# Routed transposes inside a second stage, a third first-layer PSUM buffer, moved loads and stores around the start of the dense stage, and a state copy on ScalarE, in a graph-network and expert kernel

## The chip, the cores and the metric

The kernel runs on one core of a Trainium2 chip. The core has five engines with an instruction queue each: TensorE (PE in the profile; its weight loads are shown apart as PEld), VectorE (DVE), ScalarE (ACT), GpSimd (POOL) and SyncE (SP), which here only issues DMAs. Matmul results go to PSUM, which has eight banks, and an engine must copy them out. The metric is the device time of one execution in microseconds (us), lower is better; the median of three runs is compared.

## The reference

The layer has two parts. A graph network on 128 graphs of 128 nodes with 256 features, and then a mixture of experts whose gate comes from graph attention over a million random edges. In short (N = 16384 nodes; reshapes left out):

```python
# part 1: graph network, D = 256, hidden 512
h = (1.0 + eps) * ln(x) + einsum('bnm,bmd->bnd', adj, ln(x))
x = x + relu(h @ W1 + b1) @ W2 + b2
# part 2: attention decides the experts
y = ln(x)
hg = (y @ W_gat).reshape(N, 4, 4)               # heads x experts
e = leaky_relu((hg * att_src).sum(-1)[src] + (hg * att_dst).sum(-1)[dst], 0.2)
ee = exp(e - segment_max(e, dst)[dst])
alpha = ee / (segment_sum(ee, dst)[dst] + 1e-16)
agg = segment_sum(hg[src] * alpha[:, :, None], dst) + b_gat
scores = ln(agg).reshape(N, 4, 4).mean(1)
top_s, top_i = top_k(scores, 2); w = softmax(top_s)
for ei in range(4):
    g = where(top_i == ei, w, 0).sum(-1)
    x = x + g[:, None] * (gelu(y @ W1[ei] + b1[ei]) @ W2[ei] + b2[ei])
```

Each node uses two of the four experts. All data are float32.

## The kernel before

**Stage 1** is the graph network. 32 tiles of four graphs are loaded, normalised, multiplied by their adjacency (L2091), sent through the first layer (`hidden`, matmul L2104, four blocks of 128 hidden units, two matmuls each, accumulated in a PSUM tile `p_hid` that ScalarE empties with a relu at L2108) and the second layer (`outputs`, L2115, sum on DVE at L2120), then normalised again and transposed (`turned`, L2134, also into `p_hid` tiles), and turned into the table of attention rows (`rows`, L2145). The pool `gnn_hid` holds two `p_hid` tiles. A framework schedules this stage: it orders the instructions of all engines itself. On DVE it mixes in `sort_edges`, which sorts the edges by target; its first loads are `sv` and `dv` (L226, L227) on SP's queue, and its first DVE instruction is L244.

**Stage 2** is written by hand: under `manual_schedule` the order in which the program issues instructions is the order on each engine. A small planner (`Plan`) decides this order at build time. It holds three lists of tasks, named pool, tensor and vector, each a Python generator that issues some instructions and then yields an assumed time in us, or a condition (`plan.after(us)`, `plan.was(name)`) before which it isn't to go on. The planner always steps the list whose assumed clock is furthest behind. `plan.done(name, after)` sets the time from which a condition holds. These are assumptions, nothing of them is measured on the chip: they decide order alone.

- The tensor task is `Experts.task`. Until `todo` is empty it runs 36 dense units (`dense`: tiles 23 to 31 with each of the four experts): first layer in `first` (L1614, gelu L1618), second layer in `second` (L1633, result copy on ScalarE L1640), store of the result `ys`. A unit's second layer is issued after the first layer of the next unit (`last`), so two units overlap.
- Then it runs 49 routed units. Each has two sets of 128 nodes, one set for each expert of a pair. POOL gathers their rows (`r_x`, L889), PE transposes them (`Routed.turn`, four instructions at L1760, into a tile of the pool `moe_big`), ScalarE copies the result to `m_xn` (L1764), and `Routed.load` issues the loads of the first-layer weights of the two experts on SP (L1731, L1737). `Routed.first` is the first layer (32 matmuls, L1779, gelu L1785); the second layer is again L1633 and L1640; DVE scales and adds (L1802, L1812), and POOL scatters the rows to the output (`put`, L896). `turn` does nothing if the planner doesn't yet hold the unit's rows to have arrived, if one transposed unit is already waiting, or if the list of the unit isn't there.
- The lists of nodes for the units come in five parts, of 11, 10, 10, 6 and 12 units, each built on DVE and PE from the gates of a part of the graphs (`lists`, matmuls L1440 and L1525).
- After each second layer `gathers.mark()` lets ScalarE copy a number into `marks` (L885). POOL copies it to `seen` (L880) before it issues further gathers, so that POOL doesn't run far ahead of PE.
- The vector tasks are the count of the edges (`count`, with the histogram at L738 to L776 and matmuls L761), the attention (`attend`, 13 blocks of edge rows), the sums at the ends of each node's edges (`ends`, `fetch`), and the gates (`pieces`). A block of `attend` does exponentials on ScalarE (L1141, L1142), products on DVE (L1146), a scan on DVE (L1154), a copy of the scan's states into row order on DVE (L1160), and stores of these rows on SP (L1163).

At the start of stage 2 the program issues, in this order: the load of the experts' second biases for all rows (`b2_rows`, 512 KB, L2202, SP), the first dense activations (`m_xn`, 512 KB, L1605, POOL's queue, since nothing is loaded yet), twelve small stores of zeros behind the ends of the state tables (L2237, SP); and with the first dense unit the activations of the second tile (SP).

Of the kernel before, what the change touches and what calls it, by code (L numbers as in the profile page):

```python
# [13 lines left out]
F32 = mybir.dt.float32  # L14
# [8 lines left out]
PSUM = bass.MemoryType.PSUM  # L23
DRAM = bass.MemoryType.DRAM

P = 128
D = 256
DH = 512
NB = 128
# [4 lines left out]
X = 4  # L34
# [32 lines left out]
TURN_US = 0.8  # L67
# [51 lines left out]
WIN = 16  # L119
# [17 lines left out]
ROW = 24  # L137
# [932 lines left out]
def attend(nc, c, plan, gathers, states, dst_t, aw, once, ps, ahead):  # L1070
# [11 lines left out]
    for k in range(NBL):  # L1082
# [8 lines left out]
        e = once.tile([P, H, CB + 1], F32, name="e")  # L1091
# [5 lines left out]
        else:  # L1097
            dt, st = before
# [21 lines left out]
        st = aw.tile([P, ROW, CB + 1], F32, name="state")  # L1120
# [36 lines left out]
        )  # L1157
        rows = once.tile([P, CB * ROW], F32, name="room")
        rows = rows.rearrange("p (c f) -> p c f", f=ROW)
        nc.vector.tensor_copy(rows, st[:, :, 1:].rearrange("p f c -> p c f"))  # L1160
        for (_, of), to in sorted(zip(PARTS, states), key=lambda v: v[0][1].stop):
            if of.start <= cols.start and cols.stop <= of.stop:
                nc.sync.dma_start(  # L1163
# [3 lines left out]
                    rows,  # L1167
                )
        before = (dt, st)
        yield 6.5  # L1170
        plan.done(f"states{k}", 4.0)


def finish_attention(nc, c, plan, name, graphs, hm, own, fin, aw):
# [411 lines left out]
class Experts:  # L1586
# [12 lines left out]
    def load(self, t, xn=None):  # L1599
        if t < NT and t not in self.loaded:  # L1600
            if xn is None:
                xn = self.mp.tile([P, 2, G * P], F32, name="m_xn")

            queue = self.nc.sync if self.loaded else self.nc.gpsimd
            queue.dma_start(xn, self.xn_d[t].rearrange("p (k n) -> p k n", k=2))  # L1605
            self.loaded[t] = xn

    def first(self, xn, w1, b1):
# [33 lines left out]
    def dense(self):  # L1642
        w = self.w
        t, e = self.todo.pop(0)
        self.load(t)
        if e == 0:
            self.load(t + 1)
        hid = yield from self.first(self.loaded[t], w.w1[:, e], w.b1[:, e])

        def second():  # L1650
            y = self.mp.tile([P, G, D], F32, name="m_out", bufs=3)
            yield from self.second(hid, [w.w2[:, e]] * 2, [w.b2[:, e]] * 2, y)
            self.stored.append((t, e))
            self.nc.sync.dma_start(self.ys[t, e], y.rearrange("p s d -> p (s d)"))
            self.plan.done(f"stored{t}-{e}", SECOND_US / G + 4.0)

        return second
# [8 lines left out]
    def task(self):  # L1666
        self.load(self.todo[0][0])
        yield self.plan.after(NET_US - 6.0)
        last = None
        while self.todo or last or self.routed is None or self.routed.left():  # L1670
            second = None
            self.ask()
            if not self.todo and self.routed and self.routed.turn():
                yield TURN_US
            if self.routed and self.routed.turned and not self.todo:
                second = yield from self.routed.first()
                if self.routed.turn():
                    yield TURN_US
            elif self.todo:
                second = yield from self.dense()  # L1680
            if last:
                yield from last()
                self.gathers.mark()
                yield SECOND_US / G
            elif not second:
                yield self.plan.after(0.5)
            last = second
# [149 lines left out]
def adj_ffn_kernel(  # L1837
# [22 lines left out]
    nc = tc.nc  # L1860
    ctx.enter_context(nc.allow_non_contiguous_dma(reason="weights, vectors and cells"))

    const = ctx.enter_context(tc.tile_pool(name="const", bufs=1))
# [6 lines left out]
    last = dram.tile([P, CB * ROW], F32, name="last")  # L1870
# [3 lines left out]
    states = [  # L1874
        dram.tile([NB * (cols.stop - cols.start) + WIN, ROW], F32, name=f"states{i}")
        for i, (_, cols) in enumerate(PARTS)
    ]
# [6 lines left out]
    c = Consts()  # L1884
# [70 lines left out]
    def layer_norm(work, xt, name):  # L1955
# [28 lines left out]
    right = ctx.enter_context(ExitStack())  # L1984
    mw = right.enter_context(tc.tile_pool(name="mw", bufs=1, side="right"))
    w = Consts()
# [1 line left out]
    w.ones3 = mw.tile([3, P], BF16, name="ones3")  # L1988
    nc.vector.memset(w.ones3, 1.0)
    w.b2 = mw.tile([3, X, D], BF16, name="mb2")  # L1990
    ps_one = right.enter_context(
        tc.tile_pool(name="ps_one", bufs=1, space=PSUM, side="right")
    )
    kept_pool = right.enter_context(ExitStack())
    kept = kept_pool.enter_context(tc.tile_pool(name="kept", bufs=1, side="right"))
    c.counted_raw = kept.tile([P, EC // 2], I32, name="counted")
# [12 lines left out]
    with tc.tile_pool(name="gw", bufs=1) as gw, tc.tile_pool(  # L2009
        name="gnn", bufs=2  # L2010
    ) as gp, tc.tile_pool(name="gnn_big", bufs=2, space=PSUM) as ps_big, tc.tile_pool(
        name="gnn_hid", bufs=2, space=PSUM
    ) as ps_hid, tc.tile_pool(name="gnn_small", bufs=1, space=PSUM) as ps_small:

        self_w = gw.tile([P, 1], F32, name="self_w")
# [83 lines left out]
        def hidden(h_t):  # L2099
            hid = gp.tile([P, DH // P, G * P], F32, name="hid")  # L2100
            for f in range(DH // P):
                p_hid = ps_hid.tile([P, G * P], F32, name="p_hid")
                for k in range(2):
                    nc.tensor.matmul(  # L2104
                        p_hid, w1_sb[:, k, f * P : (f + 1) * P], h_t[:, k, :],
                        start=(k == 0), stop=(k == 1),
                    )
                nc.scalar.activation(hid[:, f, :], p_hid, AF.Relu, bias=b1_sb[:, f : f + 1])  # L2108
            return hid
# [47 lines left out]
        for t in range(NT):  # L2157
            xt, h_t = sums
            hid = hidden(h_t)
            if t == 0:  # L2160
                load_row_weights()
            if t + 1 < NT:
                sums = gather_rows(*load(t + 1))
            if t > 1:
                xn_t = turned(t - 2, made.pop(0))
            x1 = outputs(t, xt, hid)
            made.append(x1)
            if t > 1:
                rows(t - 2, xn_t)
            if t == 12:  # L2170
                load_late(x1[:, 0, 0:1])
            if t == 24:

                zeros = const.tile([P, G, 2], F32, name="zeros")
                nc.vector.tensor_single_scalar(
                    zeros, x1[:, :, 0:2], 0.0, op=ALU.mult
                )
                for to in xr_tiles:
                    nc.sync.dma_start(to[:, :, 2 * D :], zeros)
        for t in (NT - 2, NT - 1):  # L2180
            rows(t, turned(t, made.pop(0)))

# [10 lines left out]
    with tc.tile_pool(name="moe", bufs=2) as mp, tc.tile_pool(  # L2193
        name="moe_big", bufs=2, space=PSUM
    ) as ps_big, tc.tile_pool(name="moe_hid", bufs=3, space=PSUM) as ps_hid, tc.manual_schedule(
        engines={ENG.DVE, ENG.Activation, ENG.PE, ENG.Pool}
    ):
        plan = c.plan = Plan()
        c.ps_big, c.ps_one = ps_big, ps_one
        first = mp.tile([P, 2, G * P], F32, name="m_xn")  # L2200
        w.b2_rows = mp.tile([P, X, D], F32, name="b2_rows", bufs=1)
        nc.sync.dma_start(w.b2_rows, b2[None].to_broadcast([P, X, D]))  # L2202
        tail = ExitStack()
        pool_fin = tail.enter_context(tc.tile_pool(name="fin", bufs=2))
        behind = tail.enter_context(ExitStack())
# [22 lines left out]
        def count():  # L2228
# [1 line left out]
            count_pool.close()  # L2230
            kept_pool.close()
            plan.done("counts")

        pad = const.tile([WIN, ROW], F32, name="no_rows")
        nc.gpsimd.memset(pad, 0.0)
        for to in states:
            nc.sync.dma_start(to[NB * (to.shape[0] // NB) :], pad)  # L2237

        def ends():

# [34 lines left out]
        def pieces():  # L2275
# [3 lines left out]
                tc.tile_pool(name="wins", bufs=2, side="right")  # L2279
            )  # L2280
            routes = Routes(nc, c, plan, fp, ps_one, xr)
            nc.sync.dma_start(hm, table[M - 1 : M, :].to_broadcast([P, ROW]))
            for i, graphs in enumerate(PIECES):
                n = graphs.stop - graphs.start
# [494 lines left out]
```

## Time and profile before

| | us |
|---|---|
| runs of the kernel before | 2299.92, 2304.63, 2306.51 |
| median | 2304.63 |
| the profiled execution | 2292.6 |
| its span (first to last instruction) | 2290.8 |
| mean clock granted to TensorE in it, as a share of full speed | 0.932 |

The profile is one execution. A group of instructions is shown by line, engine, operation, output and inputs by the program's names, and shape; then busy time in us and the mean of one in ns; then the idle time of the engine just before them and what ended most of it. Some groups that the change touches:

```profile
L1779 PE MATMUL m_phid<-m_xn,mw 128*128 128x256 f32 x1568 | 392.6, 409 | 108.3 <-ACT m_xn L1764 83.2
L1640 ACT COPY m_out<-big 128x1024 f32<-128x1024 f32 x85 | 86.0, 1012 | 559.1 <-PE big L1633 306.9
L2104 PE MATMUL p_hid<-h_t,w_sb 128*128 128x512 f32 x512 | 235.2, 608 | 21.5 <-ACT hid L2108 20.2
L2108 ACT ACTIVATE hid<-p_hid,b_sb 128x512 f32<-128x512 f32 x128 | 86.6, 681 | 67.4 <-PE p_hid L2104 67.0
L880 POOL COPY seen<-marks 128x1 f32<-128x1 f32 x85 | 26.0, 305 | 347.4 <-ACT marks L885 347.2
```

Read the first as: 1568 matmuls of the routed first layer were busy for 392.6 us, 409 ns each; PE idled 108.3 us just before them, and 83.2 of that ended when ScalarE finished writing `m_xn` at L1764.

The stretches of the span: stage 1 runs from 0 to 655, the dense units and the sort of counts from 662 to about 1027, the histogram with dense units beside it and the first gates from there to about 1301, and the routed units from 1301 to 2264. The last 27 us are result copies and sums.

### The profile page before, as it was taken

The page shows a single profiled execution, that of the slowest core. Times are in us where ns is not written, and L with a number is a line of the kernel's source. Part 1 is how long each engine was busy: PE and PEld are TensorE (multiplying, and loading weights), DVE is VectorE, ACT ScalarE, POOL GpSimd, SP SyncE. Part 2 cuts the span into 40 slices and gives each one's busy share as a digit, 9 for nine tenths or more (in the row PEclk, how much of TensorE's full clock was granted, in tenths as well). Part 3 has the DMA queues.
Part 4 walks back from the last instruction along what each step waited for, and adds up shares of the span by engine and source line. Part 5 has one row for each costly group of instructions (what it writes and reads, how often), then busy time and mean ns, then how long its engine had stood idle before and what let it go on. Part 6 is the DMA issues. An engine that isn't in the chain of part 4 may idle for free. (4 is left out here: it accounts for less than half of the span.)

```text
span 2290.8 us, 28852 instructions
## 1 busy us (share of the span) xinstructions
PE 1965.9 (86%) x8888; PEld 1466.4 (64%) x8888; DVE 1608.1 (70%) x4428; ACT 842.0 (37%) x1565; POOL 1050.6 (46%) x1011
## 2 busy tenths in 40 slices
PE   7999989988979998996698789776887977789996
PEld 4677767766756655664454468555676756667885
DVE  5889999958999998884344336464553565487877
ACT  6778545544422222322222324222232322324342
POOL 2111011101038887885455756555656654544431
PEclk9999999999979998998898899888998988899998
DMA  8898987898321122222113633453353533445866
GB/s 206 227 230 219 247 211 196 202 176 148 98 70 53 53 55 94 93 93 65 33 47 69 225 88 111 132 164 99 98 161 103 174 93 79 86 152 160 316 222 228
DMA packets 300935, 319.23 MB, mean 139 GB/s; under 512 B 112722, under 2 KB 238946, under 8 KB 300646
## 3 DMA queue, kind: packets, MB, share of 16 engines
q1 hardware_dynamic: 233030, 237.34, 33.3%
q0 software_dynamic: 67744, 79.96, 17.8%
q8 instruction: 75, 1.23, 0.2%
q14 instruction: 86, 0.70, 0.1%
HBM read 165.04 MB, written 128.04 MB: 128 GB/s over the span
## 5 line engine op out<-in xcount | busy, mean ns | idle before, releaser
L889 POOL DMA_INDIRECT hs<-table,index x552 | 624.5, 1131 | 168.0 <-issue 164.1
L1633 PE MATMUL big<-mw,m_hid 128*128 (+1 forms) x2720 | 647.3, 393 | 52.8 <-issue 52.2
L1633 PEld LDWEIGHTS big<-mw,m_hid 128*128 128x128 f32 x2720 | 524.7, 196 | 150.2 <-issue 80.8
L1779 PE MATMUL m_phid<-m_xn,mw 128*128 128x256 f32 x1568 | 392.6, 409 | 108.3 <-ACT m_xn L1764 83.2
L1779 PEld LDWEIGHTS m_phid<-m_xn,mw 128*128 128x128 f32 x1568 | 316.7, 205 | 169.0 <-ACT m_xn L1764 89.5
L1640 ACT COPY m_out<-big 128x1024 f32<-128x1024 f32 x85 | 86.0, 1012 | 559.1 <-PE big L1633 306.9
L1614 PE MATMUL m_phid<-m_xn,mw 128*128 128x512 f32 x576 | 264.1, 609 | 24.5 <-ACT m_hid L1618 12.2
L1785 ACT ACTIVATE m_hid<-m_phid,r_b 128x256 f32<-128x256 f32 x392 | 161.8, 472 | 309.7 <-remote 116.3
L2104 PE MATMUL p_hid<-h_t,w_sb 128*128 128x512 f32 x512 | 235.2, 608 | 21.5 <-ACT hid L2108 20.2
L2033 POOL DMA_DIRECT2D at<-in_adj_dram x31 | 41.0, 1324 | 432.3 <-DMA at<-self_eye 426.8
L2115 PE MATMUL big<-w_sb,hid 128*128 128x256 f32 x1024 | 228.8, 381 | 0.0
L2115 PEld LDWEIGHTS big<-w_sb,hid 128*128 128x128 f32 x1024 | 192.4, 191 | 24.6
L1614 PEld LDWEIGHTS m_phid<-m_xn,mw 128*128 128x128 f32 x576 | 110.9, 195 | 149.4 <-issue 127.6
L880 POOL COPY seen<-marks 128x1 f32<-128x1 f32 x85 | 26.0, 305 | 347.4 <-ACT marks L885 347.2
L2104 PEld LDWEIGHTS p_hid<-h_t,w_sb 128*128 128x128 f32 x512 | 94.9, 193 | 136.1 <-issue 98.2
L1618 ACT ACTIVATE m_hid<-m_phid,mb 128x512 f32<-128x512 f32 x144 | 97.5, 687 | 144.0 <-PE m_phid L1614 97.9
L889 POOL DMA_INDIRECT r_x<-xr,nodes x98 | 106.5, 1087 | 66.4 <-issue 42.8
L1540 DVE TENSOR_SCALAR low<-wide,part 128x128 bf16<-128x128 bf16 x332 | 61.3, 260 | 92.7 <-remote 34.2
L896 POOL DMA_INDIRECT out_dram<-r_x,places x98 | 105.3, 1074 | 35.0 <-issue 21.3
L1812 DVE SCALAR_TENSOR_TENSOR r_x<-m_out,r_x 128x256 f32<-128x256 f32 x196 | 90.6, 483 | 33.5 <-ACT m_out L1640 24.8
L2108 ACT ACTIVATE hid<-p_hid,b_sb 128x512 f32<-128x512 f32 x128 | 86.6, 681 | 67.4 <-PE p_hid L2104 67.0
L1802 DVE SCALAR_TENSOR_TENSOR r_x<-b_rows,r_x 128x256 f32<-128x256 f32 x196 | 90.5, 483 | 10.5 <-issue 4.8
(405 smaller groups left out, 2614.5 us busy)
## 6 DMA issues: line engine op xcount, KB each, us to landing
mw<-in_L_ffn_W_dram SPq DMA_DIRECT2D x106, 512.0 KB
states<-room SPq DMA_DIRECT2D x54, 552.0 KB
ys<-m_out SPq DMA_DIRECT2D x36, 512.0 KB
y_in<-ys SPq DMA_DIRECT2D x36, 512.0 KB
xt<-in_x_dram SPq DMA_DIRECT2D x32, 512.0 KB
xt<-b_sb POOLq DMA_DIRECT2D x32, 512.0 KB
x_d<-x SPq DMA_DIRECT2D x32, 512.0 KB
xn_d<-xn_t SPq DMA_DIRECT2D x32, 512.0 KB
```

What stands on the lines that cost most here:

```text
L889: self.nc.gpsimd.indirect_dma_start(out=out, out_offset=None, in_=rows, in_offset=bass.IndirectOffsetOnAxis(ap=index, axis=0),)
L896: sc = self.nc.gpsimd.indirect_dma_start(out=rows, out_offset=bass.IndirectOffsetOnAxis(ap=index, axis=0), in_=values, in_offset=None, bou ...
L1614: nc.tensor.matmul(p_hid, w1[:, k, f * P : (f + 1) * P], xn[:, k, :], start=(k == 0), stop=(k == 1),)
L1618: nc.scalar.activation(hid[:, f, :], p_hid, AF.Gelu, bias=b1[:, f : f + 1])
L1633: nc.tensor.matmul(p_y[:, s, :], hid[:, f, s * P : (s + 1) * P], w2[s // 2][:, f, :], start=(f == 0 and not b2), stop=(f == DH // P - 1 an ...
L1779: nc.tensor.matmul(p_hid[:, half], w1[i][:, k, f * P : (f + 1) * P], xt[:, k, :], start=(k == 0), stop=(k == 1),)
L1785: nc.scalar.activation(hid[:, f, half], p_hid[:, half], AF.Gelu, bias=b1[i][:, f : f + 1])
L1802: self.nc.vector.scalar_tensor_tensor(x[:, s, D : 2 * D], b2[i], x[:, s, 2 * D + i : 2 * D + i + 1], x[:, s, D : 2 * D], op0=ALU.mult, op1 ...
L1812: self.nc.vector.scalar_tensor_tensor(x[:, s, D : 2 * D], y[:, 2 * i + s, :], x[:, s, 2 * D + i : 2 * D + i + 1], x[:, s, D : 2 * D], op0= ...
L2104: nc.tensor.matmul(p_hid, w1_sb[:, k, f * P : (f + 1) * P], h_t[:, k, :], start=(k == 0), stop=(k == 1),)
L2108: nc.scalar.activation(hid[:, f, :], p_hid, AF.Relu, bias=b1_sb[:, f : f + 1])
L2115: nc.tensor.matmul(p_y[:, s, :], hid[:, f, s * P : (s + 1) * P], w2_sb[:, f, :], start=(f == 0), stop=(f == DH // P - 1),)
```

## The change

- In `Experts.task`, while a second layer is issued (`last`), the transposes of the next routed unit are tried after every quarter of it (`routed.turn()`), where before they were tried only before and after a first layer.
- The pool `gnn_hid` of stage 1 has three tiles in place of two. The PSUM bank for it comes from `ps_one`, which was opened before stage 1 and is now opened at the start of stage 2.
- The first dense activations are loaded on SP's queue. `b2_rows` is loaded in `pieces`, once the counts are done. The second tile's activations are loaded with the second dense unit and not with the first.
- The zeros behind the state tables are written in stage 1, in the program at the tile with number 24, where its framework places them as it sees fit.
- In `attend` the copy of the states into row order moves from VectorE to ScalarE. The planner issues it 4.6 + 1.5 us after the scan by its own clock, where before it followed the scan at once, and holds the stores as done 5.5 us after that.

```diff
@@ attend
-        nc.vector.tensor_copy(rows, st[:, :, 1:].rearrange("p f c -> p c f"))
+        yield 4.6
+        yield plan.after(1.5)
+        nc.scalar.copy(rows, st[:, :, 1:].rearrange("p f c -> p c f"))
...
-        yield 6.5
-        plan.done(f"states{k}", 4.0)
+        plan.done(f"states{k}", 5.5)
@@ Experts.load
-            queue = self.nc.sync if self.loaded else self.nc.gpsimd
-            queue.dma_start(xn, self.xn_d[t].rearrange("p (k n) -> p k n", k=2))
+            self.nc.sync.dma_start(xn, self.xn_d[t].rearrange("p (k n) -> p k n", k=2))
@@ Experts.dense
-        if e == 0:
+        if e == 1:
             self.load(t + 1)
@@ Experts.task
             if last:
-                yield from last()
+                for us in last():
+                    yield us
+                    if not self.todo and self.routed and self.routed.turn():
+                        yield TURN_US
                 self.gathers.mark()
@@ adj_ffn_kernel, before stage 1
-    ps_one = right.enter_context(
-        tc.tile_pool(name="ps_one", bufs=1, space=PSUM, side="right")
-    )
@@ stage 1
-        name="gnn_hid", bufs=2, space=PSUM
+        name="gnn_hid", bufs=3, space=PSUM
...
                 for to in xr_tiles:
                     nc.sync.dma_start(to[:, :, 2 * D :], zeros)
+                pad = const.tile([WIN, ROW], F32, name="no_rows")
+                nc.gpsimd.memset(pad, 0.0)
+                for to in states:
+                    nc.sync.dma_start(to[NB * (to.shape[0] // NB) :], pad)
@@ stage 2
+        ps_one = right.enter_context(
+            tc.tile_pool(name="ps_one", bufs=1, space=PSUM, side="right")
+        )
         plan = c.plan = Plan()
...
-        nc.sync.dma_start(w.b2_rows, b2[None].to_broadcast([P, X, D]))
...
-        pad = const.tile([WIN, ROW], F32, name="no_rows")
-        nc.gpsimd.memset(pad, 0.0)
-        for to in states:
-            nc.sync.dma_start(to[NB * (to.shape[0] // NB) :], pad)
@@ pieces
             routes = Routes(nc, c, plan, fp, ps_one, xr)
+            nc.sync.dma_start(w.b2_rows, b2[None].to_broadcast([P, X, D]))
             nc.sync.dma_start(hm, table[M - 1 : M, :].to_broadcast([P, ROW]))
```

## The prediction

> **What bounds the kernel now.** I read the page's busy shares first, then the stretches of the span, then what TensorE (PE) waits for, and last the timeline where the routed units run.
>
> ```profile
> PE 1965.9 (86%) x8888; PEld 1466.4 (64%) x8888; DVE 1608.1 (70%) x4428; ACT 842.0 (37%) x1565; POOL 1050.6 (46%) x1011
> ```
>
> PE is busy for 86% of the span, VectorE (DVE) for 70%, ScalarE (ACT) for only 37%. The average hides that the limit changes. Columns below: stretch in us, its length, then busy us of PE, PE weight loads, DVE, ACT and POOL, the PE clock, the DMA share and GB/s.
>
> ```profile
> 100.00:216.00 116.00, 110.62 (x528) 80.80 (x527) 101.08 (x383) 91.35 (x170) 15.67 (x12) 1.00 0.91 231
> 655.00:662.00 7.00, 0.01 (x1) 0.04 (x1) 6.62 (x45) 0.00 (x0) 0.48 (x2) 0.50 0.66 222
> 662.00:1027.00 365.00, 354.60 (x1184) 219.39 (x1185) 342.74 (x420) 103.87 (x156) 301.74 (x235) 0.97 0.23 69
> 1027.00:1301.00 274.00, 211.28 (x1205) 137.45 (x1204) 110.92 (x474) 67.38 (x94) 153.34 (x160) 0.89 0.29 77
> 1301.00:1700.00 399.00, 314.36 (x1413) 259.32 (x1412) 208.36 (x700) 115.40 (x235) 231.31 (x240) 0.89 0.40 122
> ```
>
> In stage 1 (to 655) PE, DVE and DMA are all near full. Between 662 and 1027 PE and DVE are both over 93% busy: PE runs dense expert units, DVE sorts counts and does the attention blocks, and the histogram at 1027 (L761) needs both. From 1301 on the routed units run; there only PE is close to its limit, 79% busy, and what it waits for is time lost:
>
> ```profile
> PE m_phid L1779 <- ACT m_xn L1764: 83.2, 25, 12.0
> PE p_hid L2104 <- ACT hid L2108: 20.2, 13, 5.9
> PE m_phid L1614 <- DMA states<-no_rows: 10.8, 1, 10.8
> PE big L1760 <- DMA r_x<-xr,nodes: 1.9, 2, 1.3
> ```
>
> (Total us, times, longest.) The biggest wait that one name carries is the first layer of a routed unit waiting for ScalarE to copy the transposed rows. The timeline of PE shows its form, and what a covered one looks like:
>
> ```profile
> 2187.09 0.60 PE L1760 MATMUL big<-ident,r_x 128*128 128x128 f32 x4
> 2188.93 7.17 PE L1779 MATMUL m_phid<-m_xn,mw 128*128 128x256 f32 x32 [1.24 <-ACT m_xn L1764]
> 2195.95 0.60 PE L1760 MATMUL big<-ident,r_x 128*128 128x128 f32 x4
> 2196.38 7.07 PE L1633 MATMUL big<-mw,m_hid 128*128 x32
> 2203.29 7.07 PE L1779 MATMUL m_phid<-m_xn,mw 128*128 128x256 f32 x32
> ```
>
> At 2187 the transposes (L1760) stand directly before their first layer and PE waits 1.24 us; at 2195 a second layer (L1633, 7.07 us) lies between and nothing is waited for. The 1.24 is the queue on ScalarE: it finishes the previous unit's result copy (L1640, 1012 ns) before the row copy (L1764, 588 ns).
>
> **Term 1, transposes inside a second layer: −24.8.** The built program's order of instructions says how often each form occurs. Before, 27 of 49 transposes have no second-layer matmul between themselves and their first layer; after, 7. The other 20 get 8 to 32 of the 32 matmuls (1.7 us or more, at 7.07/32 each) between. 20 × 1.24 = 24.8 us. The 0.60 of the transposes stays. Bounds: 0, if the time returns as another wait, and 24.8. The long waits in the row of 83.2 (5.76, 5.89, 11.45, 6.95, 11.99) I leave as they are: at most of them DVE, ScalarE and PE stand still together just after a burst of row gathers on POOL, and a turned tile ready earlier doesn't move that. What moves along: ScalarE's row copy now stands ahead of L1640 in its queue, the two expert weight loads of each unit (L1737) are issued up to 7 us earlier at a DMA share of 0.40, and the mark that lets POOL gather on (L885) keeps its place.
>
> **Term 2, drains: +11.3.** In the built order, transposes that stand behind 64 second-layer matmuls and directly before their first layer (the next list's rows weren't yet due, so both open second layers were run off) go from 2 to 5. Three more places where PE has nothing in hand. The trace doesn't show these three, so bounds: 0, since waits for gathered rows are 1.9 us in all; and the longest wait, 11.99. A wait also costs clock, which the same lines show:
>
> ```profile
> 1639.51 8.82 PE L1779 MATMUL m_phid<-m_xn,mw 128*128 128x256 f32 x32 [3.30 <-ACT m_xn L1764]
> 1845.30 10.02 PE L1779 MATMUL m_phid<-m_xn,mw 128*128 128x256 f32 x32 [11.99 <-ACT m_xn L1764]
> ```
>
> After 3.30 us of idling the 32 matmuls took 8.82 against 7.17, after 11.99 they took 10.02: 1.7 and 2.9 us more. Each drain is thus worth between 0 and 11.99 + 2.9 − 1.24 = 13.6 (the 1.24 is already left in the 7). I take the short row, 3.30 + 1.7 − 1.24 = 3.8, three times, because rows were waited for so little: 11.3; bounds 0 and 41.
>
> The Trainium skill, "TensorE: Matmul & The Clock Gate", section "HAM oscillation — how this bites in real kernels", says that PE's clock halves after an idle stretch of more than about 3.4 us. It speaks against this change, which trades gaps too short to lose the clock for a few that are long enough. By it a wait of 3.30 would cost no clock, the drains 6.2 and the whole 5 us less; the row, 8.82 after 3.30, is the measurement and decides.
>
> **Term 3, third first-layer buffer: −5.** PE's waits for L2108 are 20.2 us in 13. The first eleven, before 216 us, come to about 14; one of 5.93 at 486 is too long for one buffer, worth two matmuls (2 × 608 ns), and keeps some 4.7. So PE can win up to 14 + 1.2 + the small ones, about 16. The end of stage 1 and the histogram wait for DVE as well, though, and DVE's sort ends at 661.5. Only if DVE comes earlier does this count. DVE's adds wait for PE, which speaks for; its waits for input tiles (40.9 us, 21 times) at a DMA share of 0.88 to 0.91 speak against. Bounds 0 and −14; I take −5, nearer the DMA row.
>
> **Term 4, the pad stores: +2.** Twelve stores that lay at 655 behind the first dense load move, in the built order, to the head of SP's queue, before the first edge loads.
>
> ```profile
> 655.51 7.17 SPq L2237 DMA_DIRECT2D states<-no_rows  x12
> 35.69 1.23 DVE L244 SCALAR_TENSOR_TENSOR code<-dv 128x1024 int32<-128x1024 int32 x1 [14.13 <-ACT dv L242]
> ```
>
> They take 7.17 us of SP. DVE already idles 14.13 us for the first edges (second line), and these can come up to 7.2 later; behind them on SP stand the next input tiles. DVE's built order puts node work of two tiles ahead of L244, which covers most. Bounds 0 and +7.2; +2.
>
> **Term 5, first dense load: 0.** PE idles 10.84 us before the first dense matmul at 662 while three loads of 512 KB share 222 GB/s. By bytes, one alone takes 0.52 MB / 222 = 2.4 us, three 7.1, so up to 4.7 can go. But in the built order the second activation tile and the bias rows are issued right behind the first, about 0.4 us apart, so they still overlap; and until 1027 DVE decides. Without that cover it would be worth −3. Bounds −4.7 and 0.
>
> The Trainium skill, "Trainium Kernel Development and Optimization", section "Key Constraints", has loads from SP, ACT and POOL share the same 16 engines, so that another queue saves only issue time. By it the move from POOL's queue to SP's is worth one POOL issue at most; the profile has it at 0.57 us, and the sum has 0.
>
> **Term 6, state copies to ScalarE: −3.4 + 2.** L1160 ran 13 times on DVE at 1135 ns. Three lie before 1027, where DVE is 94% busy (342.74 of 365) and hands over to PE without slack: 3 × 1.135 = 3.4. The other ten lie where DVE is 40 to 60% busy: nothing. On ScalarE a copy of 1104 columns by the row of L1640 (1012 ns for 1024) takes 1.1 us; ScalarE is 28% busy there, and three buffers of PE cover one delayed gelu. Its cover gone, when the copy reaches ScalarE before DVE's scan (L1154, 2117 ns) is done, gelu, the result copy and PE stand behind: up to 2.1 us a block, 27 in all; the planner spaces it by 6.1 us after the scan's issue, so I take 0. With PE reaching the histogram after about 342 instead of 347 us of dense work, 5 us of it come later, into a stretch where PE idles 63 of 274: between 0 and +5, +2 taken.
>
> **Sum.** −24.8 + 11.3 − 5 + 2 + 0 − 3.4 + 2 = −17.9. The profiled execution took 2292.6 (span 2290.8, 1.8 around it), so 2274.7 by it. It lies 12 below the median of the three runs, 2304.63; carried there, 2286.7, say 2287.
>
> **The rivals.**
> *Larger gain.* Drains cost nothing and stage 1 gives its 14: 2304.6 − 24.8 − 14 + 2 − 3.4 + 2 = 2266. For it: row waits of 1.9 us. Against: DMA at 0.9 and DVE at 88% in stage 1.
> *No change, the routed stage is paced elsewhere.* A routed unit takes (2264 − 1301)/49 = 19.7 us where PE's own work is 7.07 + 7.07 + 0.60 = 14.7. If POOL's gathers and the lists made by DVE set this pace, the 24.8 come back as longer waits and the drains are how they look. Left are −5 + 2 − 3.4 + 2 = −4.4: 2300. For it: the engines that stop together. Against: POOL itself waits 347 us for PE's marks (L880), so it follows PE.
> *Slower, the drains.* One mechanism: at the three new drains the next rows come late, since PE now arrives at the list boundary sooner than the list, and PE idles with its clock lost. At 13.6 each, 41: −24.8 + 41 − 4.4 = +11.8, 2316. It decides from (24.8 + 4.4)/3 = 9.7 a drain, a wait of some 8.2 us. For it: waits of 11.45 and 11.99 are there already. Against: they are stops of all engines.
> *It doesn't do what it says.* The first load isn't alone in the built order; that is in term 5.
>
> **How the numbers follow.** Forecast 0.46, larger gain 0.16, no change 0.15, slower 0.23. The range goes from the larger gain to the slower rival, 2263 to 2316; the forecast's own is 2275 to 2297 (drains 0 to 22, stage 1 by ±5). A change under 0.3%, 6.9 us, can't be told from none here. Faster takes the forecast (0.44 of 0.46), the larger gain and 0.03 of no change: 0.63. Same has 0.02 of the forecast, 0.11 of no change, 0.02 of the slower rival: 0.15. Slower: 0.21 and 0.01 of no change: 0.22.
>
> **What would show it.** Right: waits of L1779 for L1764 fall from 25 to about 7 by number and the 1.24 rows go; PE's waits for L2108 fall from 20.2 under 6; no L1160 on DVE, and the histogram starts 4 to 8 us before 1027; a 7 us store row near the start. Wrong: single waits over 8 us before L1760 or L1779 at list boundaries, DVE's first wait at L244 over 18 us, or ScalarE idling before L1160 with gelu behind it.

## The result: slower by 0.8%, and the profile after

| | before | after |
|---|---|---|
| median us (18 runs each) | 2304.72 | 2323.07 |
| lowest to highest | 2296.59 to 2319.32 | 2309.42 to 2341.95 |
| profiled execution | 2292.6 | 2325.05 |
| its span | 2290.8 | 2323.3 |

The ratio after to before is 1.0077, 95% interval 1.0052 to 1.0101: 18 us slower where 18 us faster was forecast. One thing must be known to read what follows: the kernel before took 2281 to 2305 us in four comparisons and 2030 in two others (the last section shows how the traces of the two groups differ), so each run is given as a ratio to runs of before in its own comparison, and the two groups are kept apart.

PE's waits in the changed kernel (total us, times, longest). L1767 is the old L1764, L1782 the old L1779, L1763 the old L1760:

```profile
PE m_phid L1782 <- ACT m_xn L1767: 81.2, 13, 22.7
PE m_phid L1782 <- issue: 36.8, 21, 11.3
PE p_hid L2104 <- ACT hid L2108: 22.2, 12, 3.4
PE pt L1526 <- DVE high L1556: 19.9, 6, 7.9
PE m_phid L1614 <- DVE there L491: 6.6, 1, 6.6
```

The routed first layer waits 13 times in place of 25, as forecast, but for 81.2 us against 83.2: fewer waits, longer ones, up to 22.7. The first-layer wait of stage 1, 20.2 before, is 22.2. The wait of the first dense matmul got shorter, 10.8 before, 6.6 now. Outside the waits that the prediction named, the histogram's for L768 fell from 20.6 to 4.7 and the gaps put down to issue (nothing that the profile shows was waited for) moved: at L1633 from 52.2 to 30.8, at the routed first layer from 14.0 to 36.8. Stretches of the span, columns as before:

```profile
662.00:1027.00 365.00, 347.47 (x1147) 213.96 (x1148) 339.78 (x436) 107.67 (x156) 292.71 (x227) 0.96 0.25 71
1301.00:1700.00 399.00, 320.67 (x1395) 263.51 (x1396) 191.07 (x627) 126.40 (x242) 231.82 (x246) 0.87 0.42 121
1700.00:2100.00 400.00, 297.21 (x1441) 249.09 (x1438) 227.99 (x854) 114.46 (x222) 200.48 (x210) 0.85 0.41 115
```

The last of these stretches in the kernel before:

```profile
1700.00:2100.00 400.00, 319.51 (x1508) 265.97 (x1509) 240.75 (x870) 114.98 (x236) 213.19 (x224) 0.89 0.44 122
```

Some of the loss stands ahead of the routed units: the first list begins 13.6 us later in this trace (first matmul of `lists` at 1234.5 against 1220.9). The other traces of comparisons with before over 2280 have it anywhere from 1213 to 1229, so no part of the change can be made out in that. From 1301 to 1700 PE was then busy a little longer than before (320.67 against 314.36 us, for about as many matmuls), and from 1700 to 2100 for 297.21 us, where the kernel before had 319.51. Counted from 0, unit 15 is transposed 8 us earlier than before (1609.6 against 1617.7), unit 21, the first one of the third list, 36 us later (1761.1 against 1724.7), and that is not made up again. Long waits stand where nothing lies between a transpose and its first layer, and no second layer ahead of the transpose either:

```profile
1602.66 7.07 PE L1782 MATMUL m_phid<-m_xn,mw 128*128 128x256 f32 x32
1609.57 0.60 PE L1763 MATMUL big<-ident,r_x 128*128 128x128 f32 x4
1632.87 9.34 PE L1782 MATMUL m_phid<-m_xn,mw 128*128 128x256 f32 x32 [22.70 <-ACT m_xn L1767]
1788.38 8.36 PE L1782 MATMUL m_phid<-m_xn,mw 128*128 128x256 f32 x24 [15.83 <-ACT m_xn L1767]
2022.20 8.16 PE L1782 MATMUL m_phid<-m_xn,mw 128*128 128x256 f32 x27 [13.69 <-ACT m_xn L1767]
```

These are units 15, 22 and 32. In the kernel before, only units 12 and 38 stand so (11.45 and 0.97 us); in the changed kernel five do (12, 15, 22, 32 and 38; units 12 and 38 wait 0.97 each).

### The profile page after: what moved, and what is told of

The parts are those of the page before. It is cut to its first block, busy times and chain, and to the rows that moved or that the text cites. A ratio compares the mean times of both kernels' runs of the same rounds, so it can differ in the third digit from the quotient of the medians.

```text
span 2323.3 us, 28810 instructions
## 1 busy us (share of the span) xinstructions
PE 1978.7 (85%) x8888; PEld 1476.0 (64%) x8888; DVE 1593.8 (69%) x4415; ACT 867.5 (37%) x1580; POOL 1040.5 (45%) x1010
## 5 line engine op out<-in xcount | busy, mean ns | idle before, releaser
L889 POOL DMA_INDIRECT hs<-table,index x552 | 612.4, 1109 | 168.0 <-issue 163.8
L1633 PE MATMUL big<-mw,m_hid 128*128 (+1 forms) x2720 | 651.0, 395 | 31.3 <-issue 30.8
L1633 PEld LDWEIGHTS big<-mw,m_hid 128*128 128x128 f32 x2720 | 527.6, 197 | 130.2 <-issue 59.5
L1782 PE MATMUL m_phid<-m_xn,mw 128*128 128x256 f32 x1568 | 394.1, 409 | 124.7 <-ACT m_xn L1767 81.2
L1782 PEld LDWEIGHTS m_phid<-m_xn,mw 128*128 128x128 f32 x1568 | 320.3, 207 | 186.0 <-ACT m_xn L1767 87.3
L1614 PE MATMUL m_phid<-m_xn,mw 128*128 128x512 f32 x576 | 270.8, 619 | 30.6 <-ACT m_hid L1618 14.6
L2104 PE MATMUL p_hid<-h_t,w_sb 128*128 128x512 f32 x512 | 234.8, 608 | 23.3 <-ACT hid L2108 22.2
L1614 PEld LDWEIGHTS m_phid<-m_xn,mw 128*128 128x128 f32 x576 | 112.7, 198 | 160.6 <-issue 134.2
L880 POOL COPY seen<-marks 128x1 f32<-128x1 f32 x85 | 33.8, 398 | 345.1 <-ACT marks L885 343.9
L2108 ACT ACTIVATE hid<-p_hid,b_sb 128x512 f32<-128x512 f32 x128 | 85.5, 679 | 50.7 <-PE p_hid L2104 50.7
L2091 PEld LDWEIGHTS big<-at,xn 128*128 128x128 f32 x512 | 68.5, 207 | 44.6 <-ACT xn L1974 28.7
```

The lines of the kernel that those rows point to most:

```text
L889: self.nc.gpsimd.indirect_dma_start(out=out, out_offset=None, in_=rows, in_offset=bass.IndirectOffsetOnAxis(ap=index, axis=0),)
L1614: nc.tensor.matmul(p_hid, w1[:, k, f * P : (f + 1) * P], xn[:, k, :], start=(k == 0), stop=(k == 1),)
L1633: nc.tensor.matmul(p_y[:, s, :], hid[:, f, s * P : (s + 1) * P], w2[s // 2][:, f, :], start=(f == 0 and not b2), stop=(f == DH // P - 1 an ...
L1782: nc.tensor.matmul(p_hid[:, half], w1[i][:, k, f * P : (f + 1) * P], xt[:, k, :], start=(k == 0), stop=(k == 1),)
L2104: nc.tensor.matmul(p_hid, w1_sb[:, k, f * P : (f + 1) * P], h_t[:, k, :], start=(k == 0), stop=(k == 1),)
```

## The experiments

### Each part of the change alone

Four parts were put into the kernel before one at a time, in one comparison (before 2297.34). The edits are those of the change; the core of each:

```diff
# only_turn
+                for us in last():
+                    yield us
+                    if not self.todo and self.routed and self.routed.turn():
+                        yield TURN_US
# only_pads: the twelve stores of zeros, from the start of stage 2 into stage 1
# only_act
+        yield 4.6
+        yield plan.after(1.5)
+        nc.scalar.copy(rows, st[:, :, 1:].rearrange("p f c -> p c f"))
...
+        plan.done(f"states{k}", 5.5)
# only_hid3
+        name="gnn_hid", bufs=3, space=PSUM
```

> The kernel before with one part of the change alone: the transposes of routed rows tried within a second layer. Theory L (the lists set the pace of the routed units; a transpose that stands earlier wins nothing, and PE arrives sooner at places where it must wait): 2300 to 2312 where before is 2304, uncovered transposes gone from the profile, one or two waits over 10 us of the routed first layer in their place. Theory T (the 1.24 us gaps are really saved): 2280 to 2290. Theory D (the drains at the ends of lists cost more than the gaps): 2315 or more, and this part alone carries most of the 18 us lost.

> The kernel before with the twelve stores of zeros moved into stage 1 alone. Theory P (they stand at the head of SP's queue and hold up the first edge loads): DVE's first sort instruction at about 42 in place of 35.7, the end of stage 1 and the first dense matmul 5 to 8 us later, total 2309 to 2313 where before is 2304. Rival (stage 1 makes the start up again, since DMA and DVE are not always full): within 2 us of before.

> The kernel before with the state copies on ScalarE alone. Theory S (the copy takes 2.1 us there and stands in ScalarE's queue ahead of gelu and result copies, and the states are stored some 5 us later, so gates and lists come later): 2308 to 2318 where before is 2304, and the third list's first matmul (1628 before) later by 5 or more. Rival (DVE's 3.4 us before the histogram is won and ScalarE has room): 2299 to 2303.

> The kernel before with three first-layer PSUM tiles in stage 1 alone. Theory A (PE's waits there are for ScalarE, which is itself held up by VectorE, so a third tile only moves the wait): PE's waits for the relu stay at 15 us or more of 20, last stage-1 matmul within 2 us of 651, total within 3 us of before. Rival (the buffer was the limit): waits under 6 us, last stage-1 matmul at 640 to 648, total 2294 to 2300 where before is 2304.

| part alone | median us | ratio | 95% interval |
|---|---|---|---|
| only_turn | 2274.57 | 0.9904 | 0.9870 to 0.9938 |
| only_pads | 2296.24 | 1.0003 | 0.9982 to 1.0024 |
| only_act | 2312.44 | 1.0073 | 1.0046 to 1.0100 |
| only_hid3 | 2299.60 | 1.0009 | 0.9982 to 1.0036 |

The transposes alone bring 22 us (0.0096 × 2297). The state copies alone, with the planner's delay that came with them, lose 17. Stores and buffer can't be told from nothing. The waits of PE in only_turn, same columns:

```profile
PE m_phid L1782 <- ACT m_xn L1767: 59.4, 13, 16.8
```

13 times again, but 24 us less than in the trace of before, which is of another comparison. The stores did what was feared at the start (DVE's first sort instruction at 44.8 against 35.7, last stage-1 matmul at 657.4 against 651.2), and the whole still took the same time: six microseconds at the end of stage 1 can't be seen at the end of the kernel here. The parts sum to some −3 us with this comparison's ratios, the whole change has +18; so either two of them work against each other, or the moved loads, which this comparison lacks, lose it.

### The copy on ScalarE, or the planner's delay that came with it

The state copies differ from before in two ways: the engine, and the places of everything else, since the planner is told of a delay. Two kernels hold one of the two each.

```diff
# act_at_once
-        nc.vector.tensor_copy(rows, st[:, :, 1:].rearrange("p f c -> p c f"))
+        nc.scalar.copy(rows, st[:, :, 1:].rearrange("p f c -> p c f"))
# dve_delayed
+        yield 4.6
+        yield plan.after(1.5)
         nc.vector.tensor_copy(rows, st[:, :, 1:].rearrange("p f c -> p c f"))
...
-        yield 6.5
-        plan.done(f"states{k}", 4.0)
+        plan.done(f"states{k}", 5.5)
```

> The kernel before with the state copy on ScalarE, issued straight after the scan, without the planner's delay: the planner's order of everything else is that of before. Tells the engine from the delay. Theory E (the copy on ScalarE, 2.1 us and behind the scan, holds up gelu and result copies): as slow as the state copies alone, +12 to +20 on before. Theory O (the planner's delay of 6.1 us and its later states reorder gates, lists and gathers, and that costs): within 4 of before.

> The kernel before with the state copy left on VectorE, but issued with the planner's delay of the change (4.6 and 1.5 us, states held as done 5.5 us later). The planner's order is that of the change's state copies. Theory O: +12 to +20 on before. Theory E: within 4 of before.

> The kernel before with the transposes within a second layer and the state copies on ScalarE with their delay. If the two parts add up (-22 and +17), 5 below before. If the state copies take away what the transposes win, +10 to +20, as in the whole change; then the two parts are all of it.

> The kernel before with the loads at the start of stage 2 moved alone (bias rows later, first activations on SP, second tile with the second unit). Theory V (until the histogram VectorE decides, so PE's earlier start is worth nothing): within 3 of before, first dense matmul 2 to 5 us earlier after the last stage-1 matmul. Rival (the bias rows loaded at the counts' end collide there, or the whole change's 18 us lie here): +10 or more.

These four fell into a comparison in which before took 2030.41:

| kernel | median us | ratio | 95% interval |
|---|---|---|---|
| act_at_once | 2022.08 | 0.9960 | 0.9946 to 0.9974 |
| dve_delayed | 2031.74 | 1.0003 | 0.9991 to 1.0015 |
| turn_and_act | 2014.29 | 0.9924 | 0.9909 to 0.9939 |
| only_loads | 2026.60 | 0.9986 | 0.9975 to 0.9997 |

Here the copy on ScalarE wins 8 us, the delay costs nothing that can be seen, and transposes and copies together win 16. Neither theory's price showed. The waits in act_at_once (which keeps the old transposes) and in turn_and_act:

```profile
PE m_phid L1779 <- ACT m_xn L1764: 32.5, 27, 2.3
```

```profile
PE m_phid L1783 <- ACT m_xn L1768: 8.1, 7, 2.8
```

This is the first term of the prediction nearly alone, though the two kernels differ in the delay too: 27 uncovered transposes make 32.5 us, 7 make 8.1. Part of it comes back, as waits of the transposes for gathered rows: 8.1 us in 3 in act_at_once, 15.4 in 15 in turn_and_act. The moved loads don't lose the 18 us here. In only_loads the first dense matmul waits 6.57 us in place of 10.84. SP's queue shows that its load isn't alone: two activation loads follow each other at once, then the bias rows.

```profile
654.57 0.83 SPq L1604 DMA_DIRECT2D m_xn<-xn_d  x2
655.45 0.43 SPq L2280 DMA_DIRECT2D b_rows<-in_L_ffn_b_dram  x1
```

### The whole change with one part taken back

In a comparison with before at 2280.84 the whole change was run again, beside it without its ScalarE copy (whole_dve_copy: the `attend` of before), and the two parts in question.

> The changed kernel once more, beside its parts. The kernel before took 2030 us on one chip and 2297 to 2304 on others; the traces differ in how late TensorE's semaphore updates come while GpSimd gathers rows. Theory C (the loss depends on these late updates): on a chip without them (before near 2030) 8 to 22 below before; on one with them +14 to +22. Rival (the loss is in the order of the work): above before on either chip.

> The whole change with the state copies left on VectorE where they were. On a chip with late updates: theory S (the state copies are what loses) 18 to 26 below before, like the transposes alone; rival (pads, buffer and loads together lose) +5 or more. On a chip without them: 8 to 20 below before.

> The transposes and the state copies on ScalarE, as before on another chip (16 below before there). On a chip with late updates: if parts add up, -22 + 17 = 5 below before; if the copies eat the whole gain, +10 to +20. On a chip without: 16 below before again.

> The state copies on ScalarE alone, once more. On a chip with late updates: +12 to +20 on before as in the first run; on one without them: within 9 below and 2 above before, as the copy at once did there (-8).

| kernel | median us | ratio | 95% interval |
|---|---|---|---|
| whole_again | 2285.89 | 1.0023 | 0.9990 to 1.0056 |
| whole_dve_copy | 2258.87 | 0.9902 | 0.9870 to 0.9934 |
| turn_and_act_2 | 2289.07 | 1.0046 | 1.0018 to 1.0074 |
| only_act_2 | 2286.80 | 1.0044 | 1.0012 to 1.0075 |

Taking the state copies back turns the change into a gain of 22 us; the rest of it is sound. And the transposes bring nothing beside the state copies with their delay (1.0046 with them, 1.0044 without): the interaction that the sums asked for. The whole change lost less here than in the first result, with an interval that includes no change; between 0 and 18 us is what the runs give.

Then engine and delay were told apart again, in the whole change and alone, now with before at 2297.69. Against the change:

```diff
# whole_act_at_once
-        yield 4.6
-        yield plan.after(1.5)
         nc.scalar.copy(rows, st[:, :, 1:].rearrange("p f c -> p c f"))
...
+        yield 6.5
-        plan.done(f"states{k}", 5.5)
+        plan.done(f"states{k}", 4.0)
# whole_dve_delayed
-        nc.scalar.copy(rows, st[:, :, 1:].rearrange("p f c -> p c f"))
+        nc.vector.tensor_copy(rows, st[:, :, 1:].rearrange("p f c -> p c f"))
```

> The whole change, state copy on ScalarE, but issued straight after the scan without the planner's delay: the order of everything else is that of the whole change with the copy on VectorE, which took 0.990 of before. Theory O (the delay makes the planner put a part's window gathers behind the next block of row gathers, and the third list comes some 20 us later): 0.985 to 0.994 of before. Theory E (the 2.1 us copy on ScalarE costs): 1.000 to 1.008, like the whole change.

> The whole change with the copy left on VectorE but issued with the planner's delay: the order of the whole change without the ScalarE work. Theory O: 0.998 to 1.010 of before, like the whole change (1.002 and 1.008). Theory E: 0.985 to 0.994.

> The state copy on ScalarE at once, alone, once more. On a chip with late semaphore updates (before near 2280 to 2300): theory O within 0.997 and 1.002 of before, theory E 1.004 to 1.008. On a chip without (before near 2030): 0.996 again.

> The state copy on VectorE with the planner's delay, alone, once more. On a chip with late semaphore updates: theory O 1.003 to 1.008, theory E within 0.998 and 1.002. On a chip without: 1.000 again.

| kernel | copy on | planner's delay | median us | ratio | 95% interval |
|---|---|---|---|---|---|
| whole_act_at_once | ScalarE | no | 2275.77 | 0.9881 | 0.9839 to 0.9922 |
| whole_dve_delayed | VectorE | yes | 2309.70 | 1.0050 | 1.0021 to 1.0080 |
| act_at_once_2 | ScalarE | no | 2284.33 | 0.9938 | 0.9904 to 0.9972 |
| dve_delayed_2 | VectorE | yes | 2307.33 | 1.0028 | 0.9998 to 1.0058 |

It is the delay, beside the rest of the change. With VectorE doing the copy as before and only the planner's times changed, the whole change loses as it did; with ScalarE doing it at once the change wins 27 us (0.0119 × 2298) and beats both kernels. Alone on VectorE the delay's loss is not clear of nothing (1.0028). The waits of these two, again of the routed first layer for the row copy:

```profile
PE m_phid L1781 <- ACT m_xn L1766: 54.7, 15, 13.5
```

```profile
PE m_phid L1782 <- ACT m_xn L1767: 91.1, 13, 22.6
```

Two things go with it in the traces. The first are the lists. Times from the first list's first matmul (L1440 before), from the traces of the comparisons with before over 2280:

| kernel | planner's delay | second list begins | third list begins | last second layer ends |
|---|---|---|---|---|
| before | no | 206 | 407 | 1049 |
| only_turn | no | 206 | 406 | 1035 |
| whole_dve_copy | no | 201 | 389 | 1019 |
| whole_act_at_once | no | 203 | 398 | 1036 |
| act_at_once_2 | no | 203 | 399 | 1041 |
| only_pads | no | 201 | 403 | 1038 |
| only_hid3 | no | 203 | 405 | 1051 |
| only_act | yes | 217 | 429 | 1068 |
| dve_delayed_2 | yes | 214 | 428 | 1059 |
| only_act_2 | yes | 206 | 414 | 1057 |
| turn_and_act_2 | yes | 210 | 423 | 1044 |
| the change | yes | 210 | 426 | 1065 |
| whole_again | yes | 210 | 417 | 1050 |
| whole_dve_delayed | yes | 219 | 449 | 1069 |

In each kernel with the delay the third list begins later (414 to 449) than in any without (389 to 407). The ends overlap (1044 to 1069 with, 1019 to 1051 without), and only_turn ends 14 us sooner than before with its lists where before has them.

The second are the places where PE has nothing in hand, the drains of the prediction. In each of the four kernels with both the delay and the new transposes (turn_and_act_2, the change, whole_again, whole_dve_delayed) units 15, 22 and 32 are transposed directly between two first layers, and the three waits come to 44 to 52 us. With the new transposes but no delay (only_turn, whole_dve_copy, whole_act_at_once) none of the three stands so. PE's idle time from the first transposes to the last second layer follows: 165 to 174 us with neither, 155 to 163 with the transposes, 180 to 187 with the delay, 175 to 195 with both. In turn_and_act, where before takes 2030, the same three places wait 4.8 us together, and there the two parts win. That these waits are the loss is read from the traces; no run changes them alone.

### By which step of the planner

The built order shows one step that fits: with the delay, the gathers of the ends of edges (`win`), from which gates and lists are made, stand one part, six row gathers, later on POOL for lists two and three. Each of these two lists needs ten such gathers. Two kernels tried it.

```diff
# whole_done_early
-        plan.done(f"states{k}", 5.5)
+        plan.done(f"states{k}", 4.0)
# whole_at_once_short: the change, copy on ScalarE at once, then
+        yield 4.6
+        plan.done(f"states{k}", 4.0)
```

> The whole change with one number changed: the planner holds the states as done 4.0 us after the copy in place of 5.5. In the built order the window gathers of the second and third list go back in front of the next six row gathers (first windows of the second list after 6.39 blocks of rows again, not 6.52; of the third after 8.26, not 8.39). Theory W (the place of the window gathers sets when the lists come): 0.985 to 0.996 of before, third list's first matmul 10 us or more earlier, against the end of stage 1, than in the whole change. Rival (the delay of the copy itself, or the distance it makes elsewhere in the order): 1.000 to 1.010 as in the whole change.

> The whole change with the copy on ScalarE at once, and the planner counting 4.6 us for the rest of the block on VectorE in place of 6.5, since the copy is gone from there. Theory W: window gathers of lists two and three stay early (6.39 and 8.26), so 0.984 to 0.994 of before, like the copy at once (0.988). Rival (any new order costs some 10 us by chance): 0.995 to 1.005.

The comparison had before at 2030.77. whole_done_early: 2037.17, ratio 1.0030 (1.0014 to 1.0046); whole_at_once_short: 2010.72, ratio 0.9910 (0.9883 to 0.9937). In whole_done_early the third list began 323 us after the first, as in turn_and_act (325) and not as in act_at_once (314) or whole_at_once_short (301). Theory W's price is missed, but the test was not clean: POOL's order in the traces has six of the third list's ten window gathers back in their places and the last four still behind 398 row gathers, as in every other trace with the delay, against 392 in all ten without it. So theory W is neither shown nor excluded. The two kernels of this comparison are the cleanest pair on the delay itself: the copy is on ScalarE, the planner counts 4.6 us and the done time is 4.0 in both; the one difference is that the 4.6 us, with the 1.5 behind them, stand ahead of the copy or after it, and that is worth 26 us (2037.17 against 2010.72). The drains don't explain this pair: transposes directly between two first layers wait 7.9 us in all in whole_done_early. Where before takes 2030, moreover, turn_and_act won 16 us with its third list at 325, so the list's place alone doesn't set the time. Which step between the later copy and the loss carries it stays open, and so does how the whole change itself fares where before takes 2030: it was not run there.

## Why the prediction was wrong, by its own steps

**Term 1, −24.8: right for the transposes alone.** They brought −22, and where before takes 2030 the waits went from 32.5 to 8.1, which is 24.4. Beside the state copies with their delay they brought nothing (1.0046 against 1.0044).

**Term 2, drains, +11.3: the count was right, the size wrong.** The traces have the five places, against two, as transposes directly between two first layers, not behind 64 second-layer matmuls: those are two in the change, at units 10 and 31, with waits of 3.83 and 11.27. The three new ones wait 22.70, 15.83 and 13.69 us, 52 in all, where the term took 3.30 us of wait for each and had 41 as its upper bound. The row of 3.30 has a second layer ahead of its transpose; the two rows of this form in the kernel before waited 11.45 and 0.97. And they come only with the delay: only_turn has none of them, and the delay with the old transposes (only_act) has units 12, 22 and 34 so. The slower rival had the sign, nearly the size (2316) and the drains, for a reason that is not the one seen: the rows were gathered and transposed in time at these three, and ScalarE's copy of them started late (the last section).

**Term 3, third buffer, −5: wrong.** Alone 1.0009 (0.9982 to 1.0036). PE's waits for L2108 fell from 20.2 to 14.1, and none of it can be seen in the time; in the whole change they stayed at 22.2.

**Term 4, stores, +2.** At L244 they cost 6.3 us in the change and 9.1 alone, about the upper bound of 7.2; an effect on the whole is not to be seen.

**Term 5, first load, 0.** The wait fell by 4.3, near the bound of 4.7, and 2.8 us (0.0014 × 2030) came through, more than the 0 that I gave.

**Term 6, −3.4 + 2: the step that failed.** It costed a moved copy by the copy. The copy was mis-sized, 2.1 us against the 1.1 that I took from another row, and that did no harm:

```profile
L1162 ACT COPY room<-state x13: 2077/2123/2185, 899.4 to 2175.2; 128x1104 f32<-128x1104 f32 x13
```

(Shortest, median and longest in ns.) On ScalarE at once it wins 14 us (0.0062 × 2298) or 8 us where before takes 2030: more than the three copies before the histogram. The +2 priced something else, dense work that comes behind the histogram. The lines with the delay, which change the order on POOL, DVE and PE for the rest of the kernel, had no price of their own. The prediction used the delay as a safety ("the planner spaces it by 6.1 us after the scan's issue, so I take 0") where it was the cost: alone, on VectorE, 1.0028 with an interval that just holds 1, on ScalarE 1.0073 and 1.0044 where the copy at once has 0.9938; and beside the transposes from 0.988 to 1.005 in one comparison, 39 us, in two kernels that differ in the copy's engine too, and 26 us in the pair with one engine. So a cost taken as 0 was 26 to 39 us beside the rest of the change, and where before takes over 2280 the drains that term 2 sized at 11.3 come with it.

**The rivals.** "No change, the routed stage is paced elsewhere" named the lists, and they do come later with the delay; that they set the time is not shown, since the transposes alone won 22 us without earlier lists. I gave the rival no place where they could become later, since nothing in the diff touched them by name.

## What to carry to other kernels

In a kernel whose order is made by a planner, a changed time or condition is a change to every queue, and its price isn't that of the instruction beside it: build the order with the time alone changed and compare where the producers of later work stand. When a bundle of edits loses, run each alone and the whole with each taken back; the four singles here couldn't show that two parts undo each other. And where a change makes new places at which an engine has nothing in hand, price them by the rows of the same form in the trace, here 0.97 and 11.45 us, not by a shorter row of another form.

## What the runs showed of the hardware

**Late completions while GpSimd gathers.** From 1602.66 to 1609.6 in the change's trace PE ran the 32 matmuls of a first layer without a pause, then the transposes (the rows shown with the result). ScalarE applies gelu to each quarter of the result and copies the transposed rows; it started like this (the first row holds quarters 1 and 2):

```profile
1605.92 1.57 ACT L1788 ACTIVATE m_hid<-m_phid,r_b 128x256 f32<-128x256 f32 x4
1613.73 0.84 ACT L1788 ACTIVATE m_hid<-m_phid,r_b 128x256 f32<-128x256 f32 x2 [6.24 <-remote]
1627.17 0.84 ACT L1788 ACTIVATE m_hid<-m_phid,r_b 128x256 f32<-128x256 f32 x2 [12.60 <-remote]
1632.23 0.58 ACT L1767 COPY m_xn<-big 128x512 f32<-128x512 f32 x1 [4.23 <-remote]
```

The trace holds the updates of the semaphore, the counter that PE raises to tell the other engines that such a piece is done. Beside the ends that the profile models:

```
                     quarter 2  quarter 3  within 4  quarter 4  transposes
modelled end         1606.28    1608.01    1608.87   1609.73    1610.17
semaphore update     1606.54    1613.70    1620.07   1627.14    1632.16
```

ScalarE's starts on quarters 3 and 4 and on the transposed rows come 0.03 to 0.07 us after the updates, not after the ends. Elsewhere an update comes 15 ns after the modelled end. POOL issued row gathers and two scatters from 1600.8 to 1629.7, with gaps of 0.3 us. Updates over 2 us late appear from about 850 us on, in the stages with gathers, and they make up the 22.7 us wait shown with the result. Added up without overlap they come to between 370 and 450 us in each of the fourteen traces of the comparisons with before over 2280, as much in before as in the change; the sum depends on how updates are matched to pieces of work, since 66 to 87 of some 900 updates have no record there. The six traces of the comparisons with before at 2030 show none. There the same stretch of time looks like this (act_at_once; its routed units began 78 us earlier):

```profile
1301.00:1700.00 399.00, 369.83 (x1902) 319.03 (x1901) 280.86 (x992) 155.94 (x305) 306.16 (x315) 0.99 0.57 164
```

PE is 93% busy, against 79% before, and POOL gathers more in the same time. Kernels that ran in both groups differ by some 250 to 280 us. That the late updates make this difference fits the waits, but no run separates them from anything else that may differ. Whether it is the updates that are late or the matmuls themselves, whether the gathers cause it, and why one and the same chip showed it in one comparison and not in another, these runs can't tell.

**The clock after a gap.** Two waits in the change's trace, 3.32 and 3.83 us long:

```profile
1529.80 9.67 PE L1782 MATMUL m_phid<-m_xn,mw 128*128 128x256 f32 x32 [3.83 <-ACT m_xn L1767]
1550.13 7.17 PE L1782 MATMUL m_phid<-m_xn,mw 128*128 128x256 f32 x32 [3.32 <-ACT m_xn L1767]
```

The 32 matmuls after the shorter one took their usual 7.17 us, those after the longer one 9.67. The Trainium skill, "TensorE: Matmul & The Clock Gate", section "HAM oscillation — how this bites in real kernels", puts the limit at about 3.4 us, and this pair agrees; the row of 3.30 with 8.82 in the kernel before doesn't. Over all twenty traces there is no sharp limit. Of the routed first layer's waits with 32 unbroken matmuls behind them, these were followed by more than 8 us in place of 7.2: 1 of 96 between 1.0 and 1.3 us, 5 of 20 to 2.7, 9 of 14 to 3.4, 12 of 13 to 4.0, and all 47 above.
